# Graph attention's f column: turned in blocks on VectorE and spread over DRAM, in place of TensorE transposes

## The chip, the cores and the metric

The kernel runs on one core of a Trainium2 chip. A core has TensorE (PE: matrix products and transposes; its weight loads are shown apart as PEld), VectorE (DVE), ScalarE (ACT), GpSimd (POOL) and SyncE (SP, which here only issues transfers), each with its own instruction queue that runs in order. They share an on-chip memory of 128 partitions (SBUF); TensorE writes its results to PSUM[...]. Transfers to and from DRAM run on 16 DMA engines. The metric is the time of one execution on the device in microseconds.

## The reference, cut to what matters

There are 64 graphs with 256 nodes and 256 features each, and an adjacency matrix per graph. Four layers follow each other, each wrapped as `x = layernorm(x + layer(x, adj))`: a masked transformer layer, two graph attention layers, and a relational convolution. The change touches the two attention layers. In shortened form:

```python
h = x @ W                             # 256 x 256
f, g = h @ a[0], h @ a[1]             # two numbers for each node
s = leaky_relu(f[:, None] + g[None, :], 0.2)
s = where(adj > 0, s, -inf)
out = softmax(s, axis=-1) @ h
```

Layer 1 adds a bias, layer 2 applies elu. Every score needs one node's f and another node's g.

## The kernel before, in words

A node index is tiled as 2 blocks of 128 partitions (`NB = 2`, `P = 128`, `N = 256`). For each graph, `graph(g)` states every piece of work as an operation of a plan: its engine, an expected cost in microseconds, what it reads and writes, and the ring from which it takes a buffer. `Plan.schedule` then plays the whole program through once, with these costs and with a lag for each engine before others may use a result (for a transfer 3.5 us, unless the operation gives its own `lag`). It starts on each engine the ready operation with the earliest due time, and so writes down the order in which each engine gets its instructions. Graphs follow each other every 46 us by their due times, and the last five are drawn together; at any time several graphs are at different layers, and TensorE takes from all of them. On the chip only this order remains; waiting is done by semaphores.

The attention layer is `gat`. It transposes x (`transposed`, L602 and L605), and makes `h` by products with `gw`, whose weights carry two more columns, so that column `F_COL` of h is f and column `G_COL` is g (L625; copied out of PSUM by ScalarE at L796 in layer 2, by VectorE with a bias at L798 in layer 1). The scores are laid out transposed: keys on the partitions, queries along the free dimension. So g is one number per partition, taken as a scalar operand, and f has to stand as a row on all 128 partitions. Before, TensorE makes that row: `spread` (L807) transposes, for both blocks, the f column repeated 128 times, into a PSUM bank `pf`. VectorE then forms the scores with the mask `gm` in two steps of 128x256 (L812) and applies the leaky slope (L815), ScalarE takes the exponential (L817), and TensorE multiplies h by e (L625 again, bank<-h,e). A further column of ones in h gives the softmax's denominator.

SyncE issues the loads and stores: eight loads of `blocks` per graph for the transposed input (L615), two of `adj` and one each of `x` and `xr` (L578), and the store of the result (L923). GpSimd issues two accumulating transfers per graph (L587), and works on the small operands of the layer norms (L639 to L642). An operation may be marked as using the memory port[...] (`"uses"`), or as waiting for it (`"waits"`); the planner then keeps the marked work of the two engines apart. The turn of 32x32 blocks on VectorE is already in use once per graph, for the input (L618).

Of the kernel before, what the change touches and what calls it, by code (L numbers as in the profile page):

```python
# [17 lines left out]
P = 128  # L18
# [4 lines left out]


RINGS = {"x": 2, "adj": 4, "bits": 2, "am": 2, "gm": 6, "T": 4, "qk": 2, "v": 2, "p": 12, "both": 4, "inv": 1, "ctxT": 2, "X": 8,
         "xr": 1, "hid": 1, "h": 3, "e": 3, "n": 1, "rel": 3, "hi": 2, "lo": 2, "o": 4, "blocks": 1, "xT": 2}
SMALL = {"mv": 8, "st": 4, "rstd": 8, "r": 6, "rdeg": 4}


# [21 lines left out]
class Plan:  # L51
# [29 lines left out]
    def op(self, engine, cost, issue, graph, reads=(), writes=(), takes=(), mode=None, port=None, lag=None):  # L81


        o = Op(engine, cost, mode, graph, issue, port, lag)
        for accesses, writing in ((reads, False), (writes, True)):
            for a in accesses:
                t, part = a if isinstance(a, tuple) else (a, None)
                write = writing
                if t.ring == "bank":
                    write, part = True, None  # L90
                keys = [k for k in t.parts if part is None or k is None or k == part]
                for k in keys:
                    writer, readers = t.parts[k]
                    o.before.update(readers if write else ())
                    if writer is not None:
                        o.before.add(writer)
                if write:
                    if part is None:
                        t.parts = {}
                    t.parts[part] = (o, [])  # L100
                else:
                    for k in keys or [part]:
                        t.parts.setdefault(k, (None, []))[1].append(o)
                if t not in o.tiles and t.ring is not None:
                    o.tiles.append(t)
        o.tiles += [t for t in takes if t not in o.tiles]
        for t in o.tiles:
            t.left += 1
        o.before.discard(o)
        for b in o.before:  # L110
            b.after.append(o)
        self.ops.append(o)
# [96 lines left out]
def tile_gnn_stack(ctx: ExitStack, tc: tile.TileContext, t: dict, out: bass.AP):  # L209
# [16 lines left out]
    nc = tc.nc  # L226
    x_in, adj_in = t["x"], t["adj"]
    B, N, D = x_in.shape
# [3 lines left out]
    NB = N // P  # L232
# [6 lines left out]
    ONE, F_COL, G_COL = D + 2, D, D + 1  # L239
# [5 lines left out]
    pools = {}  # L245
# [42 lines left out]
    def rows(name, zeros=0):  # L288

        v = t[name]  # L290
        n = v.shape[0]
        w = const.tile([P, n + zeros], F32, tag=f"row_{name}", name=f"row_{name}")
        if zeros:
            nc.vector.memset(w[:, n:], 0.0)
        nc.gpsimd.dma_start(w[:, 0:n], bass.AP(tensor=v.tensor, offset=v.offset, ap=[[0, P], [1, n]]))
        return w
# [12 lines left out]
    ident = const.tile([P, P], F32, tag="ident", name="ident")  # L309
# [169 lines left out]
    def main_path(plan):  # L479
# [4 lines left out]
        def ring(name, bufs):  # L484
            plan.ring(name, bufs, lambda shape, dtype, i: pools["work"].tile(shape, dtype, tag=f"{name}{i}", name=name))
# [3 lines left out]
        for name, bufs in SMALL.items():  # L489
            ring(name, bufs)  # L490
        plan.ring("bank", 8, bank)

        c_wqkv, c_wo, c_w1, c_w2, c_b1, c_bo = (plan.fixed(w) for w in (wqkv, wo, w1, w2, b1, bo))
        c_gw, c_cw = [plan.fixed(w) for w in gw], [plan.fixed(w) for w in conv_w]
# [59 lines left out]
        def graph(g):  # L554
            def op(engine, cost, issue, reads, writes, takes=(), mode=None, port=None, lag=None):
                plan.op(engine, cost, issue, g, reads, writes, takes, mode, port, lag)

            def pe(mode, cost, issue, reads, writes, takes=()):
                op("PE", cost, issue, reads, writes, takes, mode)

            def dve(cost, issue, reads, writes, port=None):
                op("DVE", cost, issue, reads, writes, port=port)

            def act(cost, issue, reads, writes):
                op("ACT", cost, issue, reads, writes)
# [4 lines left out]
            def new(ring, shape, dtype=F32):  # L570
                return plan.tile(ring, shape, dtype)

            def tok(ring, dtype=F32):
                return new(ring, [P, NB, D], dtype)
# [20 lines left out]
            def transposed(xt):  # L595

                xT, pt = new("T", [P, KB, N]), new("bank", [P, KB, N])

                def issue():
                    for kb in range(KB):  # L600
                        for i in range(NB):
                            nc.tensor.transpose(pt()[:, kb, i * P : (i + 1) * P], xt()[:, i, kb * P : (kb + 1) * P], ident)  # L602

                pe("full", 0.44, issue, [xt], [pt], [xT])
                act(0.47, lambda: nc.scalar.copy(xT(), pt()), [pt], [xT])  # L605
                return xT
# [15 lines left out]
            def product(dst, lhs, rhs, n):  # L622

                for c in range(n):
                    nc.tensor.matmul(dst, lhsT=lhs(c), rhs=rhs(c), start=(c == 0), stop=(c == n - 1))  # L625
# [161 lines left out]
            def gat(xt, layer, gm, seen, bias, finish):  # L787
                xT = transposed(xt)
                w, c_w = gw[layer], c_gw[layer]
                h, e, z = new("h", [P, NB, HW]), tok("e"), tok("X")  # L790
                for i in range(NB):
                    ph = new("bank", [P, D + 2])
                    pe("full", 0.87, lambda i=i, ph=ph: product(ph(), lambda kb: xT()[:, kb, i * P : (i + 1) * P],
                                                                lambda kb: w[:, kb, :], KB), [xT, c_w], [ph], [h])
                    if bias is None:
                        act(0.27, lambda i=i, ph=ph: nc.scalar.copy(h()[:, i, 0 : D + 2], ph()), [ph], [(h, i)])  # L796
                    else:
                        dve(0.34, lambda i=i, ph=ph: nc.vector.tensor_tensor(h()[:, i, 0 : D + 2], ph(), bias, op=ALU.add),  # L798
                            [ph], [(h, i)])
                pool(0.1, lambda: (nc.gpsimd.memset(h()[:, :, ONE : ONE + 1], 1.0)), [xT], [(h, "one")], None)  # L800
                pool(0.2, lambda: nc.gpsimd.tensor_tensor(seen_fg[:, seen], h()[:, :, F_COL : G_COL + 1],
                                                          h()[:, :, F_COL : G_COL + 1], op=ALU.mult), [(h, 0), (h, 1)], [], "waits")
                pf = new("bank", [P, N])

                def spread():
                    for i in range(NB):
                        nc.tensor.transpose(pf()[:, i * P : (i + 1) * P],  # L807
                                            h()[:, i, F_COL : F_COL + 1].to_broadcast([P, P]), ident)

                pe("full", 0.22, spread, [(h, 0), (h, 1)], [pf], [e])  # L810
                for i in range(NB):
                    dve(0.40, lambda i=i: nc.vector.scalar_tensor_tensor(e()[:, i, :], pf(), h()[:, i, G_COL : G_COL + 1],  # L812
                                                                         gm()[:, i, :], op0=ALU.add, op1=ALU.min),
                        [pf, (h, i), gm], [(e, i)])
                dve(0.60, lambda: nc.vector.scalar_tensor_tensor(e(), e(), SLOPE, e(), op0=ALU.mult, op1=ALU.max), [e], [e],  # L815
                    "uses")
                act(0.52, lambda: nc.scalar.activation(e(), e(), AF.Exp), [e], [e])  # L817
                for i in range(NB):
                    po, r = new("bank", [P, HW]), new("r", [P, 1])
                    pe("full", 0.87, lambda i=i, po=po: product(po(), lambda kt: e()[:, kt, i * P : (i + 1) * P],  # L820
                                                                lambda kt: h()[:, kt, :], NB), [e, h], [po], [z, r])
                    dve(0.08, lambda po=po, r=r: nc.vector.reciprocal(r(), po()[:, ONE : ONE + 1]), [po], [r])
                    finish(i, z, po, r)
                return z
# [82 lines left out]
            xT = input_transposed()  # L907
            adj = load("adj", adj_graph[g], I32)
            am, gm = masks(adj)
# [8 lines left out]
            rel = relation(load("adj", adj_graph[g], I32))  # L918
            rdeg = new("rdeg", [P, NB])
            h = conv(conv(xt, 0, rel, rdeg), 1, rel, rdeg)  # L920
# [7 lines left out]
        for o in plan.schedule():  # L928
            o.issue()

    with tc.tile_pool(name="work", bufs=1) as pools["work"], tc.manual_schedule():
        main_path(Plan())


# [180 lines left out]
    with tc.tile_pool(name="general", bufs=1) as pools["work"], tc.If(wrong > 0):  # L1115
# [11 lines left out]
        with tc.For_i(0, G) as g:  # L1127
            xt = load(gen, x_view[bass.ds(g, 1)], F32, "x")
            xr = load(gen, x_view[bass.ds(g, 1)], F32, "xr")
# [56 lines left out]
```

## Time and profile before

| | |
|---|---|
| median of 3 runs | 2942.13 us (2940.86 to 2942.64) |
| profiled run, span | 2939.3 us |
| TensorE busy | 2894.3 us (98%) |
| VectorE busy | 2415.6 us (82%) |
| ScalarE busy | 1585.1 us (54%) |
| GpSimd busy | 861.4 us (29%) |
| TensorE clock granted | 0.997 of full speed |
| DMA, mean | 49 GB/s |

The span is the time from first to last instruction in the profile. Busy is the time in which at least one instruction of the engine was running. A matrix instruction is pipelined, so its duration from start to end overlaps that of the next one; what the queue pays for it is the distance from its start to the next start. Products in 32-bit floats appear as two records of TensorE for one instruction of the program; transposes appear as one. Lines such as L807 are lines of the kernel's text.

### The profile page before, as it was taken

Reading aid. Unit: us, or ns where it says so; the run is one execution under the profiler, and the core shown is the slowest. Engines: PE = TensorE matmul, PEld = TensorE weight load, DVE = VectorE, ACT = ScalarE, POOL = GpSimd, SP = SyncE. Lnnn points to the kernel's source line nnn. Section 1 sums busy time; section 2 is a strip of 40 time slices with the busy share of each in tenths; the row PEclk is TensorE's granted clock in tenths of the full one; section 3 lists DMA queues with packets and bytes.
Section 4 is the critical chain, followed back from the end, with each engine's and each line's share of the span. In section 5 each row is a group of like instructions: output and inputs, shape, how many; then the busy total and the mean of one; then the engine's idle time right before and its main releaser. Section 6 shows DMA issues by size and latency. Waiting matters only on the chain.

```text
span 2939.3 us, 50120 instructions
## 1 busy us (share of the span) xinstructions
PE 2894.3 (98%) x17206; PEld 2224.7 (76%) x17206; DVE 2415.6 (82%) x6172; ACT 1585.1 (54%) x3841; POOL 861.4 (29%) x2005
## 2 busy tenths in 40 slices
PE   8999999999999999999999999999999999999997
PEld 6777777777777777777777778777777777777884
DVE  6788887888878888878888788878878888889778
ACT  3555554554555556556555555555555555556454
POOL 2233232332322323223233222222332223323232
PEclk9999999999999999999999999999999999999999
DMA  7221121222212222212122212121221212212100
GB/s 179 46 55 44 40 58 38 50 51 47 48 38 51 48 50 44 58 33 58 44 48 48 43 44 62 40 51 44 51 51 40 55 33 51 54 44 48 33 15 23
DMA packets 266037, 143.99 MB, mean 49 GB/s; under 512 B 146960, under 2 KB 264976, under 8 KB 265776
## 3 DMA queue, kind: packets, MB, share of 16 engines
q1 hardware_dynamic: 230336, 105.96, 13.8%
q0 software_dynamic: 35440, 34.76, 8.2%
q8 instruction: 139, 2.28, 0.3%
q14 instruction: 122, 1.00, 0.1%
HBM read 90.32 MB, written 16.78 MB: 36 GB/s over the span
## 4 chain that ended last, share of the span: by engine, by line
PE 84%; DVE 8%; POOL 3%; ACT 2%; issue 1%; DMA 1%; SPq 1%; POOLq 0%; DVEq 0%; ACTq 0%
PE bank L625 66%; PE bank L602 4%; PE bank L887 4%; PE bank L744 3%; PE bank L719 3%; PE bank L739 2%; POOL rstd L640 1%; DVE st L634 1%; ACT X L646 1%; PE bank L807 1%; DVE o L897 1%; DVE X L760 1%; DVE mv L636 1%; DVE p L727 1%; POOL rstd L639 0%
## 5 line engine op out<-in xcount | busy, mean ns | idle before, releaser
L639 POOL TENSOR_SCALAR rstd<-mv 128x2 f32<-128x2 f32 x384 | 108.5, 282 | 1323.0 <-DVE mv L636 1139.2
L625 PE MATMUL bank<-T,w 128*128 128x256 f32 x2048 | 480.0, 380 | 1.1 <-ACT T L605 1.1
L646 ACT ACTIVATE X<-X,rstd 128x256 f32<-128x256 f32 x640 | 349.8, 597 | 231.4 <-POOL rstd L642 164.7
L625 PE MATMUL bank<-cw,T 128*128 128x512 f32 x1024 | 463.6, 595 | 3.7 <-ACT T L605 2.9
L625 PE MATMUL bank<-w,hid 128*128 128x256 f32 x2048 | 462.5, 380 | 0.0
L625 PEld LDWEIGHTS bank<-w,hid 128*128 128x128 f32 x2048 | 383.6, 190 | 54.7 <-issue 4.0
L625 PEld LDWEIGHTS bank<-T,w 128*128 128x128 f32 x2048 | 378.1, 190 | 59.7 <-issue 8.8
L625 PEld LDWEIGHTS bank<-cw,T 128*128 128x128 f32 x1024 | 191.0, 190 | 200.9 <-issue 181.6
L727 DVE TENSOR_TENSOR p<-p,am 128x512 f32<-128x512 f32 x512 | 331.0, 681 | 10.8 <-ACT p L725 10.6
L725 ACT ACTIVATE p<-bank 128x512 f32<-128x512 f32 x512 | 299.1, 596 | 46.4 <-PE bank L719 46.0
L640 POOL TENSOR_TENSOR rstd<-rstd,neghalf 128x2 f32<-128x2 f32 x384 | 303.7, 791 | 32.0
L777 ACT ACTIVATE hid<-bank,col_b 128x256 f32<-128x256 f32 x512 | 213.0, 472 | 117.9 <-PE bank L625 116.2
L625 PE MATMUL bank<-xT,wqkv 128*128 128x256 f32 x1024 | 252.8, 386 | 12.8 <-DVE xT L618 11.5
L605 ACT COPY T<-bank 128x512 f32<-128x512 f32 x320 | 185.1, 586 | 144.2 <-PE bank L602 141.4
L625 PE MATMUL bank<-gw,T 128*128 128x258 f32 x1024 | 249.2, 383 | 1.6 <-ACT T L605 1.5
L625 PE MATMUL bank<-h,e 128*128 128x259 f32 x1024 | 249.0, 383 | 0.9 <-ACT e L817 0.3
L634 DVE BATCH_NORM_STATS2 st<-X 128x6 f32<-128x256 f32 x640 | 237.4, 413 | 1.7
L874 ACT CAST hi<-bank 128x256 fp32r<-128x256 f32 x256 | 94.8, 370 | 256.7 <-PE bank L625 256.1
L748 DVE RECIPROCAL inv<-bank 128x256 f32<-128x256 f32 x128 | 218.7, 1732 | 12.2 <-PE bank L744 12.2
L625 PEld LDWEIGHTS bank<-xT,wqkv 128*128 128x128 f32 x1024 | 188.2, 191 | 49.0 <-DVE xT L618 11.5
L625 PEld LDWEIGHTS bank<-h,e 128*128 128x128 f32 x1024 | 190.5, 190 | 45.8 <-issue 18.4
L625 PEld LDWEIGHTS bank<-gw,T 128*128 128x128 f32 x1024 | 189.7, 190 | 40.0 <-issue 9.1
(120 smaller groups left out, 4997.3 us busy)
## 6 DMA issues: line engine op xcount, KB each, us to landing
adj<-in_adj_dram SPq DMA_DIRECT2D x128, 256.0 KB, 2.8
blocks<-in_x_dram SPq DMA_DIRECT2D x512, 32.0 KB, 2.0
x<-in_x_dram SPq DMA_DIRECT2D x64, 256.0 KB, 2.9
xr<-in_x_dram SPq DMA_DIRECT2D x64, 256.0 KB, 2.7
xr<-row_ln_b POOLq DMA_DIRECT2D x64, 256.0 KB, 4.1
x<-row_bo POOLq DMA_DIRECT2D x64, 256.0 KB, 4.1
out_dram<-o SPq DMA_DIRECT2D x64, 256.0 KB, 2.2
w<-in_W1T_dram SPq DMA_DIRECT2D x1, 1024.0 KB, 12.3
```

The costliest lines, as they stand in the source:

```text
L602: nc.tensor.transpose(pt()[:, kb, i * P : (i + 1) * P], xt()[:, i, kb * P : (kb + 1) * P], ident)
L605: act(0.47, lambda: nc.scalar.copy(xT(), pt()), [pt], [xT])
L625: nc.tensor.matmul(dst, lhsT=lhs(c), rhs=rhs(c), start=(c == 0), stop=(c == n - 1))
L634: nc.vector.bn_stats(stat()[:, i, :], y()[:, i, :])
L639: nc.gpsimd.tensor_scalar(rstd()[:, 0, :], mv()[:, :, 1], 1.0, EPS, op0=ALU.mult, op1=ALU.add)
L640: nc.gpsimd.tensor_tensor(rstd()[:, 0, :], rstd()[:, 0, :], neghalf[:, 0:NB], op=ALU.pow)
L646: nc.scalar.activation(y()[:, i, :], y()[:, i, :], AF.Identity, bias=rstd()[:, 1, i : i + 1], scale=rstd()[:, 0, i : i + 1])
L725: act(0.58, lambda pr=pr, k=k, sr=s[r]: nc.scalar.activation(pr(), sr(), AF.Exp, accum_out=seen_sum[:, k : k + 1]), [s[r]], [pr])
L727: dve(0.60, lambda pr=pr, kt=kt: nc.vector.tensor_tensor(pr(), pr(), am()[:, kt, None, :].to_broadcast([P, KB, N]), op=ALU.mult), [pr, am] ...
L748: dve(1.62, lambda hg=hg, pc=pc: nc.vector.reciprocal(inv()[:, hg, :], pc()[:, 1, :]), [pc], [(inv, hg)])
L777: act(0.36, lambda f=f, k=k, ph=ph: nc.scalar.activation(hid()[:, f + k, :], ph()[:, k, :], AF.Relu, bias=b1[:, f + k : f + k + 1]), [ph, ...
L887: nc.tensor.matmul(pa()[:, 0:n], lhsT=rel()[:, i, j * P : (j + 1) * P], rhs=part()[:, i, 0:n], start=(c == 0), stop=(c == len(terms) - 1))
```

## The change

The row of f is no longer made by TensorE. VectorE turns the f column of each of h's two blocks, repeated 32 times, in blocks of 32x32 into a tile `own` (128 x 64 in all). In it, partition 32 b + r holds f of the nodes 32 b to 32 b + 31 of the block, the same for each r. Two transfers by SyncE write the two halves to a DRAM tile `f_row` of 32 x 256, in which each of the 32 rows is then the whole f. A third reads it back to the tile `f` on 128 partitions, 32 rows four times over. The score step reads f from SBUF and no longer from a PSUM bank[...]. The planner is told a lag of 2.2 us for each write and 4.3 us for the read, in place of its 3.5. The buffer of `e` is taken at the first score step; before, it was taken at the transposes. The rings `f`, `own` and `f_row` have two buffers each. The planner orders all engines' instructions anew with this.

```diff
-         "xr": 1, ..., "o": 4, "blocks": 1, "xT": 2}
+         "xr": 1, ..., "o": 4, "blocks": 1, "f": 2, "own": 2, "xT": 2}
+DRAM = {"f_row": 2}
...
-                pf = new("bank", [P, N])
-                def spread():
-                    for i in range(NB):
-                        nc.tensor.transpose(pf()[:, i * P : (i + 1) * P],
-                                            h()[:, i, F_COL : F_COL + 1].to_broadcast([P, P]), ident)
-
-                pe("full", 0.22, spread, [(h, 0), (h, 1)], [pf], [e])
+                own, rows, pf = new("own", [P, NB * 32]), new("f_row", [32, N]), new("f", [P, N])
+                def turn():
+                    for i in range(NB):
+                        nc.vector.transpose(own()[:, i * 32 : (i + 1) * 32], h()[:, i, F_COL : F_COL + 1].to_broadcast([P, 32]))
+
+                dve(0.22, turn, [(h, 0), (h, 1)], [own], "uses")
+                for i in range(NB):
+                    op("SP", 0.51, lambda i=i: nc.sync.dma_start(rows()[:, i * P : (i + 1) * P].rearrange("r (b n) -> b r n", b=4),
+                                                                 own()[:, i * 32 : (i + 1) * 32]), [own], [(rows, i)], lag=2.2)
+                op("SP", 0.54, lambda: nc.sync.dma_start(pf(), rows()[None, :, :].to_broadcast([4, 32, N])), [rows], [pf], lag=4.3)
                 for i in range(NB):
                     dve(0.40, lambda i=i: nc.vector.scalar_tensor_tensor(e()[:, i, :], pf(), h()[:, i, G_COL : G_COL + 1],
                                                                          gm()[:, i, :], op0=ALU.add, op1=ALU.min),
-                        [pf, (h, i), gm], [(e, i)])
+                        [pf, (h, i), gm], [(e, i)], "uses")
```

More of the change, by code (lines that the diff above doesn't have):

```diff
@@ L25 @@
 RINGS = {"x": 2, "adj": 4, "bits": 2, "am": 2, "gm": 6, "T": 4, "qk": 2, "v": 2, "p": 12, "both": 4, "inv": 1, "ctxT": 2, "X": 8,
-         "xr": 1, "hid": 1, "h": 3, "e": 3, "n": 1, "rel": 3, "hi": 2, "lo": 2, "o": 4, "blocks": 1, "xT": 2}
+         "xr": 1, "hid": 1, "h": 3, "e": 3, "n": 1, "rel": 3, "hi": 2, "lo": 2, "o": 4, "blocks": 1, "f": 2, "own": 2, "xT": 2}
+DRAM = {"f_row": 2}
 SMALL = {"mv": 8, "st": 4, "rstd": 8, "r": 6, "rdeg": 4}
@@ L491, in main_path @@
         plan.ring("bank", 8, bank)
+        for name, bufs in DRAM.items():
+            plan.ring(name, bufs, lambda shape, dtype, i, name=name: pools["dram"].tile(shape, dtype, tag=f"{name}{i}", name=name))
         c_wqkv, c_wo, c_w1, c_w2, c_b1, c_bo = (plan.fixed(w) for w in (wqkv, wo, w1, w2, b1, bo))
@@ L929, in main_path @@
             o.issue()
-    with tc.tile_pool(name="work", bufs=1) as pools["work"], tc.manual_schedule():
+    with (tc.tile_pool(name="work", bufs=1) as pools["work"],
+          tc.tile_pool(name="dram", bufs=1, space=bass.MemoryType.DRAM) as pools["dram"], tc.manual_schedule()):
         main_path(Plan())
```

## The prediction, made before the changed kernel was run

> **What bounds the kernel now.** I read the busy table and the slices first, then TensorE's and VectorE's busy time by stretch, the chain of waits, and last the groups and one stretch in order of time around the two transposes that go.
>
> ```profile
> span 2939.3 us, 50120 instructions
> PE 2894.3 (98%) x17206; PEld 2224.7 (76%) x17206; DVE 2415.6 (82%) x6172; ACT 1585.1 (54%) x3841; POOL 861.4 (29%) x2005
> ...
> PE 84%; DVE 8%; POOL 3%; ACT 2%; issue 1%; DMA 1%; SPq 1%; POOLq 0%; DVEq 0%; ACTq 0%
> ```
> ```profile
> 100.00:2800.00 2700.00, 2685.44 (x16068) 2065.07 (x16067) 2239.99 (x5681) 1475.19 (x3588) 797.92 (x1838) 1.00 0.22 47
> 2800.00:2880.00 80.00, 79.65 (x383) 63.82 (x382) 63.60 (x201) 42.87 (x92) 24.03 (x80) 1.00 0.04 8
> 2880.00:2939.30 59.30, 43.67 (x183) 26.10 (x181) 48.41 (x152) 26.01 (x55) 13.09 (x36) 0.93 0.08 28
> ```
> Columns of the second: stretch, length, then busy us of PE, PEld, DVE, ACT, POOL, the granted clock, the DMA share, GB/s. From 100 to 2800 us TensorE idles 14.6 us of 2700. It is the bound, and a microsecond taken from its queue is a microsecond of span, as long as nothing makes it wait. VectorE has 17% to spare there. Only the last 59 us are different: TensorE 74% busy, VectorE 82%.
>
> What the removed work costs, from the group and then in order of time (start, length):
> ```profile
> L807 PE MATMUL bank<-ident,h 128*128 128x128 f32 x256 | 49.6, 275 | 0.5 <-ACT T L605 0.5
> ...
> 1456.56 0.28 PE L887 MATMUL bank<-hi,rel 128*128 128x256 f32 x1
> 1456.68 0.38 PE L807 MATMUL bank<-ident,h 128*128 128x128 f32 x2
> 1456.89 3.62 PE L625 MATMUL bank<-w,hid 128*128 128x256 f32 x16
> ```
> The 275 ns is one transpose from start to end, and 49.6 us the group's union; both overlap their neighbours. What the queue pays is start to next start: 1456.89 - 1456.68 = 0.21 us for a pair; the pairs at 2871.74 and 2881.67 give 0.22.
>
> What waits for it, and what SyncE has pending:
> ```profile
> DVE e L812 <- PE bank L807: 33.7, 27, 5.4
> ...
> SPq L923 <- ACT o L646: 275.4, 47, 30.5
> ```
> ```profile
> blocks<-in_x_dram SPq DMA_DIRECT2D x512, 32.0 KB, 2.0
> x<-in_x_dram SPq DMA_DIRECT2D x64, 256.0 KB, 2.9
> ```
> Last column: us to landing.
>
> [...] the trace has only the 128x512 one (703 ns). [...] 474 ns for the step with the bank as source, 415 for L843 from SBUF. [...]
>
> **The change, part by part.**
> *Removed:* 2 layers x 64 graphs = 128 pairs x 0.215 us = 27.5 us of TensorE time, all in the saturated part: -27.5. The PSUM bank of the row also falls away; TensorE does not wait for banks before, so 0.
> *VectorE:* 256 turns of 128x32. Not in the trace. From below: the 128x32 memset, 85 ns. [...] I take 0.1 us of queue each (tails overlap), 26 us. The score step now reads SBUF: 256 x (474 - 415) = 15 us less. Net +11 us, bounds +7 to +37, on 2415 with over 500 idle: hidden beside TensorE, 0. [...] the planner keeps GpSimd's small work off them; that work (29% busy) has room.
> *SyncE:* 384 more transfers at some 0.39 us of issue (the trace's median for a load) = 150 us, in a queue that mostly waits. The traffic is 128 x (32 + 128) KB = 21 MB more on 144; the DMA share is 0.22. Hidden, 0. Past what they are moved: loads of blocks, adj, x, xr and the stores, in program order. Counted in the changed program, 69 of 128 row loads have another transfer between the row's writes and its load, mostly a load of blocks; 7 have a store, which waits for ScalarE.
> *The new wait:* from the end of the second h product to the first h x e product. Before, in the stretch above: copy of h to 1456.30 (0.7 us after the products), then the transposes, and 2.8 us from the first score step (1457.28) to the end of the exponential (1460.08). Now, in place of the transposes: turns 0.4, two writes 2 x 0.39 + 2.0, the load 0.39 + 2.7 (the low value for 256 KB), in all 6.3; with what the planner is told (2 x 0.51 + 2.2 + 0.54 + 4.3, and the turns) 8.5. Chain 0.7 + 6.3 + 2.8 = 9.8 us, or 12.0. Against it stands the TensorE work that the new order puts between: I counted its instructions there and priced each by the spacing in the timeline (product of 256 columns 0.434 us, of 512 0.86, transpose 0.11, gather 0.118). Median 14.6 us in the first 116 layers (7 before), 15 of them under 13 and 3 under 12, lowest 9.6. So the chain fits with 2.6 to 4.8 us to spare; I put 2 us in all for the few tight ones (0 to 15).
> *Behind that wait:* VectorE is in order. Between turn and score step lie 7.5 us of its own work at the median, but under 4 in a tenth of the layers; there it stands, and masks, normalisations and the copies of lo behind it stand with it. Its 17% idle pays for that.
> *The end:* of the last 12 layers four have 7.4, 6.1, 8.3 and 7.8 us of TensorE work against a chain of 9.8. The first waits 2.4; the second contains this wait and waits 1.3 more; the third contains both; the last waits 2.0. Sum 5.7 us, with the long chain 14: +6.
> *Start:* the first layer comes at 65 us with 13.6 us of work: 0.
> *Buffers:* h (ring of 3) is held some 7 us longer, twice in a graph's 46 us: room. f, own and f_row have two each, with 23 us between layers.
>
> Sum: -27.5 + 2 + 6 = -19.5, so 2919.8 on the profiled span of 2939.3. The times are some 2.8 us above that span (2942.13 median): 2922.6.
>
> **Rivals.**
> *A, slower: SyncE's order makes the row late.* SyncE's queue is in order and often stands: 47 waits for ScalarE averaged 5.9 us. If one such wait stands ahead of a row's write or load, the row is late, VectorE stops at the score step, and TensorE after it. It decides when TensorE waits over 27.5/128 = 0.21 us per layer beyond what I count, thus once the row takes some 3 us more than planned as a rule. A wait of 1.5 us in a third of the layers costs 64 us: 2942 - 27.5 + 6 + 64 = 2985. For it: 15 row writes stand directly behind a store, 28 behind a load of xr (one buffer). Against: the planner issues a transfer only when it thinks its buffer free, and no load of the before kernel makes TensorE wait after the start.
> *B, no change:* the tail gives 14 and the tight layers 13: 2942. For it: the tail's VectorE is nearly full. Against: it needs the upper end of two terms at once.
> *C, larger gain:* the pair is worth its group's union, 49.6 us: 2942 - 50 + 8 = 2900. Against: the starts, 0.21 us apart, three times.
> *D, the change does nothing for the bound,* VectorE taking over: 2415 + 37 = 2452 us, far under 2890. Out.
>
> **How the numbers follow.** Main case 0.70 (own range 2910 to 2935), C 0.06, B 0.08, A 0.16. Predicted 2923. The range 2905 to 2945 leaves out most of A and half of C. What a measurement of this kernel tells from no change is about 0.2%, 5.9 us: faster 0.76, same 0.08, slower 0.16.
>
> **What would show it.** Right: TensorE's busy time near 2867 us; idle between 100 and 2750 us still under 20 us; score steps on VectorE waiting for the row's transfer in some layers without TensorE waiting; the row's load landing in 2.5 to 4.5 us, its writes in 2; turns at 0.1 to 0.2 us; the score step at about 415 ns; a few microseconds of TensorE idle some 100 us before the end. Wrong: the h x e product on TensorE waiting for the exponential in many layers, with SyncE's row writes behind stores or buffer waits (A), or an end stretch longer by over 10 us (B).

## The result, and the profile after

The changed kernel takes 2954.73 us (median of 4 runs, 2952.18 to 2955.82) against 2941.49 before, a ratio of 1.0044 with a 95% interval of 1.0027 to 1.0061. It is slower by some 13 us, outside the predicted range and of the opposite sign.

The page of the changed kernel, its span, busy table and the chain that ended last:

```profile
span 2953.4 us, 50442 instructions
PE 2886.7 (98%) x16950; PEld 2205.0 (75%) x16950; DVE 2437.8 (83%) x6428; ACT 1583.9 (54%) x3841; POOL 894.7 (30%) x2005
...
PE 81%; DVE 9%; POOL 3%; ACT 3%; issue 2%; DMA 1%; SPq 1%; POOLq 0%; DVEq 0%; ACTq 0%
```

TensorE has 256 records less, as meant, but it is busy only 7.6 us less, where 27.5 were expected, and its idle time (span less busy) has grown from 45.0 to 66.7 us. By stretch, with the columns of the prediction's table:

```profile
100.00:2800.00 2700.00, 2669.68 (x15818) 2040.90 (x15817) 2258.18 (x5911) 1474.02 (x3591) 828.55 (x1839) 1.00 0.24 54
2800.00:2880.00 80.00, 73.52 (x323) 58.76 (x322) 53.47 (x177) 34.66 (x73) 23.46 (x71) 0.94 0.14 31
2880.00:2953.40 73.40, 57.88 (x236) 35.39 (x235) 61.66 (x199) 35.18 (x74) 16.36 (x46) 0.94 0.09 28
```

The steady stretch, which had 14.6 us of TensorE idle, has 30.3. The last product of the transformer layer's scores marks where the end begins, since no new graph enters after it. Here it is before and after (count, shortest, median and longest duration in ns, first and last start):

```profile
L719 PE MATMUL bank<-qk x2048: 373/374/479, 19.1 to 2745.5; 32*128 32x256 f32 x187
```
```profile
L722 PE MATMUL bank<-qk x2048: 374/374/479, 19.8 to 2749.0; 32*128 32x256 f32 x187
```

Up to it the change lost 3.5 us, where some 25 should have been won. From it to the end it went from 193.8 to 204.4 us, 10.6 more.

Whom TensorE waits for, before and after (us in total, times, longest). X is the tile that a layer norm leaves for the next layer:

```profile
PE bank L602 <- ACT X L646: 3.6, 8, 1.3
```
```profile
PE bank L605 <- ACT X L649: 18.7, 33, 1.6
...
PE bank L628 <- ACT e L825: 3.4, 3, 2.0
```

It is not the exponential of the scores (e, 3 waits), behind which the row stands. The largest entry is X, 33 times in place of 8: 15.1 us more, of the 21.7 us by which TensorE's idle time grew. VectorE does stand for the row, but seldom:

```profile
DVE e L820 <- DMA f<-f_row: 19.5, 15, 5.2
```

One stretch with waits for X, 1274 to 1289 us, on TensorE and then GpSimd, in order of time (start, length; in brackets the idle time before it):

```profile
1282.38 2.00 PE L628 MATMUL bank<-xT,wqkv 128*128 128x256 f32 x8
1285.42 0.33 PE L605 MATMUL bank<-ident,X 128*128 128x128 f32 x1 [1.05 <-ACT X L649]
1285.91 0.55 PE L605 MATMUL bank<-ident,X 128*128 128x128 f32 x3 [0.16 <-ACT X L649]
...
1288.32 0.33 PE L605 MATMUL bank<-ident,X 128*128 128x128 f32 x1 [1.64 <-ACT X L649]
```
```profile
1282.98 0.19 POOL L642 TENSOR_SCALAR rstd<-mv 128x2 f32<-128x2 f32 x1 [1.85 <-DVE mv L639]
1283.25 0.70 POOL L643 TENSOR_TENSOR rstd<-rstd,neghalf 128x2 f32<-128x2 f32 x1
1284.03 0.20 POOL L644 TENSOR_TENSOR rstd<-mv,rstd 128x2 f32<-128x2 f32 x1
1284.31 0.19 POOL L645 TENSOR_SCALAR rstd<-rstd 128x2 f32<-128x2 f32 x1
1284.58 0.64 POOL L642 TENSOR_SCALAR rstd<-mv 128x2 f32<-128x2 f32 x1
1285.31 1.03 POOL L643 TENSOR_TENSOR rstd<-rstd,neghalf 128x2 f32<-128x2 f32 x1
1286.41 0.62 POOL L644 TENSOR_TENSOR rstd<-mv,rstd 128x2 f32<-128x2 f32 x1
1287.12 0.51 POOL L645 TENSOR_SCALAR rstd<-rstd 128x2 f32<-128x2 f32 x1
```

GpSimd makes the reciprocal root of a layer norm in four small steps, and ScalarE then makes X with it. Two roots follow each other. The first takes 1.5 us (1282.98 to 1284.50), the second 3.05 us, and X comes after it. On VectorE, meanwhile:

```profile
1284.52 2.46 DVE L730 TENSOR_TENSOR p<-p,am 128x512 f32<-128x512 f32 x4
1286.90 2.49 DVE L734 TENSOR_TENSOR both<-p 128x512 f32<-128x512 f32 x4
```

These are steps with two SBUF inputs, and GpSimd's steps are longer beside them in this trace: the first step of a root (L642) takes 191 ns where it overlaps no step of VectorE (median of 57, at most 193) and 542 ns where it overlaps p<-p,am most (median of 40). Where it overlaps the score step most, it took 191 ns before, when that step read f from a bank (35, at most 193), and takes 331 ns now, with f in SBUF (12). The doubled root agrees with that. It is not shown to be the cause of the waits: the same pair of roots stands ahead of the waits at 1652 and 2016 us, but ahead of that at 793 us the root took 1.7 us, and the kernel before also has roots of over 2.5 us (42 of 384; the changed kernel has 52). VectorE is full in the whole stretch (DVE in the first line below), and the statistics of three layer norms end on it one behind the other from 1281.9 to 1284.6 us:

```profile
1274.00:1288.40 14.40, 11.55 (x81) 8.64 (x79) 14.37 (x43) 10.81 (x29) 8.73 (x17) 1.00 0.24 73
1289.00:1292.40 3.40, 3.40 (x10) 2.77 (x10) 1.14 (x3) 2.29 (x6) 2.54 (x7) 0.51 0.98 145
```

The second line is what comes next: for 3.4 us the granted clock (third number from the end) is 0.51. The starts of TensorE's product records stand 0.43 us apart there, against 0.22 us at 1273 to 1276 us, so work takes twice as long. The trace's record of the clock has 7 such stretches, 27.3 us in all, between the start-up and the last product of the changed kernel; the kernel before has none. Five lie in the steady stretch, each behind waits for X; of the two in the end, one follows a wait for X and one the longest wait for e. Up to 13.7 us of the missing 19.9 us of busy time is this (an estimate, from 27.3/2).

### The profile page after: what moved, and what is told of

Read it like the earlier page. It is cut to its first block, busy times and chain, and to the rows that moved or that the text cites. A ratio compares the mean times of both kernels' runs of the same rounds, so it can differ in the third digit from the quotient of the medians.

```text
span 2953.4 us, 50442 instructions
## 1 busy us (share of the span) xinstructions
PE 2886.7 (98%) x16950; PEld 2205.0 (75%) x16950; DVE 2437.8 (83%) x6428; ACT 1583.9 (54%) x3841; POOL 894.7 (30%) x2005
## 4 chain that ended last, share of the span: by engine, by line
PE 81%; DVE 9%; POOL 3%; ACT 3%; issue 2%; DMA 1%; SPq 1%; POOLq 0%; DVEq 0%; ACTq 0%
PE bank L628 65%; PE bank L605 4%; PE bank L895 4%; PE bank L747 3%; PE bank L722 3%; PE bank L742 2%; POOL rstd L643 1%; DVE st L637 1%; ACT X L649 1%; DVE X L763 1%; DVE inv L751 1%; DVE mv L639 1%; POOL rstd L645 1%; POOL rstd L644 1%; ACT p L728 1%
## 5 line engine op out<-in xcount | busy, mean ns | idle before, releaser
L642 POOL TENSOR_SCALAR rstd<-mv 128x2 f32<-128x2 f32 x384 | 114.9, 299 | 1498.8 <-DVE mv L639 1326.9
L628 PE MATMUL bank<-T,w 128*128 128x256 f32 x2048 | 471.8, 381 | 0.7 <-ACT T L608 0.6
L730 DVE TENSOR_TENSOR p<-p,am 128x512 f32<-128x512 f32 x512 | 334.1, 679 | 18.6 <-ACT p L728 18.3
L643 POOL TENSOR_TENSOR rstd<-rstd,neghalf 128x2 f32<-128x2 f32 x384 | 316.0, 823 | 32.0
L751 DVE RECIPROCAL inv<-bank 128x256 f32<-128x256 f32 x128 | 219.3, 1733 | 22.6 <-PE bank L747 22.2
L628 PEld LDWEIGHTS bank<-xT,wqkv 128*128 128x128 f32 x1024 | 186.9, 191 | 51.3 <-DVE xT L621 12.7
```

The costliest lines, as they stand in the source:

```text
L642: nc.gpsimd.tensor_scalar(rstd()[:, 0, :], mv()[:, :, 1], 1.0, EPS, op0=ALU.mult, op1=ALU.add)
L643: nc.gpsimd.tensor_tensor(rstd()[:, 0, :], rstd()[:, 0, :], neghalf[:, 0:NB], op=ALU.pow)
L730: dve(0.60, lambda pr=pr, kt=kt: nc.vector.tensor_tensor(pr(), pr(), am()[:, kt, None, :].to_broadcast([P, KB, N]), op=ALU.mult), [pr, am] ...
L751: dve(1.62, lambda hg=hg, pc=pc: nc.vector.reciprocal(inv()[:, hg, :], pc()[:, 1, :]), [pc], [(inv, hg)])
```

## The experiments

The theories: **R**, the row comes late (the prediction's rival A); **V**, VectorE's added work, and what it holds up on GpSimd; **O**, the new order of all instructions is worse by itself, within it **M**, through the marks, and **L**, through the lag; **C**, every order is its own draw. Each run is compared with the kernel before, measured beside it (median 2941.5 beside the changed kernel, 2942.9 to 2943.5 beside the others), so differences of 2 to 3 us between rows are not to be relied on. "X waits" are TensorE's waits for a normalised X in the profile (us, times; the kernel before has 3.6, 8). Runs e1, e3, e4, e8 and e11b leave out the row, so their output lacks f.

| run | us | ratio to before, 95% | X waits |
|---|---|---|---|
| changed kernel | 2954.7 | 1.0044 [1.0027, 1.0061] | 18.7, 33 |
| e1 row not read | 2956.1 | 1.0044 [1.0027, 1.0060] | 18.6, 32 |
| e3 order alone | 2949.5 | 1.0023 [1.0013, 1.0034] | 18.3, 35 |
| e5 no marks | 2940.7 | 0.9990 [0.9983, 0.9997] | 7.1, 15 |
| e7 score mark only | 2963.3 | 1.0065 [1.0048, 1.0082] | 14.7, 25 |
| e7b turn mark only | 2950.0 | 1.0022 [1.0015, 1.0029] | 12.0, 25 |
| e8 order alone, no marks | 2939.3 | 0.9983 [0.9974, 0.9991] | 9.8, 18 |
| e9 no marks, shorter lags | 2958.1 | 1.0049 [1.0032, 1.0066] | 10.7, 27 |
| e13 changed, VectorE less | 2948.2 | 1.0016 [1.0009, 1.0023] | 17.3, 33 |
| e4 before, no transposes | 2929.1 | 0.9953 [0.9936, 0.9969] | 5.0, 13 |
| e11 before, VectorE less | 2941.8 | 0.9995 [0.9986, 1.0004] | 2.7, 6 |
| e11b e4, VectorE less | 2926.0 | 0.9938 [0.9921, 0.9954] | 5.2, 12 |
| e6 before, score step marked | 2945.7 | 1.0008 [0.9999, 1.0016] | 7.7, 23 |
| e10 before, other cost | 2945.8 | 1.0005 [0.9997, 1.0014] | 2.8, 9 |
| e12 no marks, last six as before | 2928.5 | 0.9951 [0.9934, 0.9968] | 4.2, 11 |
| e14 the same with marks | 2950.2 | 1.0023 [1.0013, 1.0032] | 15.8, 27 |
| e15 no marks, last nine as before | 2923.7 | 0.9937 [0.9921, 0.9954] | 2.9, 10 |

**Is it the wait for the row?** e1 keeps the changed kernel's plan and all its transfers; only the score step reads something else.

```diff
-  nc.vector.scalar_tensor_tensor(e()[:, i, :], pf(), h()[:, i, G_COL : G_COL + 1],
+  nc.vector.scalar_tensor_tensor(e()[:, i, :], no_f, h()[:, i, G_COL : G_COL + 1],
```


> The changed kernel in its own order, with turns, writes and the load of f all issued, but the score step (VectorE) reads a constant row of zeros in place of f, so that nothing waits for the transfers; the output then lacks f. Changed kernel: 2954.7 us, before: 2941.5. Theory R (the row comes late: VectorE stands 19.5 us in 15 waits for it, and everything behind it on VectorE too): at most 2935, since the waits and most of the 13.7 us that half-clock stretches cost go. Theory O (the new order of all instructions is itself worse; the waits for the row are not what delays TensorE): 2948 to 2957. Theory V (more work on VectorE[...]): 2948 to 2957 too.

2956.1 us, as the changed kernel, with VectorE's 15 waits for the row gone. R has fallen: these waits cost nothing that can be measured, in the end either (204.5 us after the last scores product, against 204.4).

**Is it the order?** e3 also leaves out the turns and the three transfers, in the same plan. Its score step reads the constant row, as in e1 (that edit is not shown again).

```diff
-  dve(0.22, turn, [(h, 0), (h, 1)], [own], "uses")
+  dve(0.22, lambda: None, [(h, 0), (h, 1)], [own], "uses")
   ...
-  op("SP", 0.51, lambda i=i: nc.sync.dma_start(rows()[...], own()[...]), [own], [(rows, i)], lag=2.2)
+  op("SP", 0.51, lambda: None, [own], [(rows, i)], lag=2.2)
```


> As the run with the row not read, and neither turns nor writes nor the load of f are issued: what is left of the change is the removal of TensorE's transposes and the new order. Theory O: 2942 to 2955, slower than or equal to before although TensorE has 27.5 us less to do. Theory V: the 256 turns (0.2 us each from start to end, 51 us as a group's sum at most) and their traffic are gone, so 2915 to 2930. Theory R: the same as the run with the row not read, at most 2935.

2949.5 us: with TensorE's transposes gone and nothing put in their place, the kernel is still slower than before. Its waits for X are those of the changed kernel. The added work thus costs 5 to 7 us (2954.7 and 2956.1 to 2949.5), and the order all the rest. O stands, V only for these few us.

```profile
PE bank L606 <- ACT X L650: 18.3, 35, 1.6
```

**What are the transposes worth?** e4 takes them out of the kernel before and leaves its order alone; its score step too reads a constant row.

```diff
-  pe("full", 0.22, spread, [(h, 0), (h, 1)], [pf], [e])
+  pe("full", 0.22, lambda: None, [(h, 0), (h, 1)], [pf], [e])
```


> The kernel before in its own order, with TensorE's two transposes of f not issued; the score step reads a constant row of zeros from SBUF (output lacks f). It tests the first term of the prediction, 128 pairs x 0.215 us = 27.5 us of a saturated queue: 2914 if each microsecond taken from TensorE is one of span in the old order (all of O, R and V allow it; O needs it). If it is over 2930, the price itself was wrong, since other engines hold TensorE back in any order.

2929.1 us, between the two bounds: a gain of 13.8 us on the 2942.9 of before in this comparison, half of the price. e3 and e4 issue the same number of instructions on every computing engine and differ in the plan that ordered them; the new order alone thus costs 20.4 us. The waits for X in e4 are few:

```profile
PE bank L603 <- ACT X L647: 5.0, 13, 1.4
```

The price itself holds: in the trace of before, the distances from each of the 256 transposes to the next start sum to 31.0 us, with a median of 0.218 us for a pair. In e4, TensorE's busy time is 18.0 us lower than in the profile before and its idle time 6.3 us higher (51.3 against 45.0). Its record of the clock has two stretches at half clock more than before ahead of the end, 6.8 us in the start-up and 3.4 us at 1562 us; they account for up to 5.1 us of the busy time that did not go (an estimate, half of their length).

e11 and e11b ask whether VectorE takes the other half. e11 is the kernel before, e11b is e4, both without the checking step of the relation (L857), 64 of 128x512, so the count that it keeps stays zero.

```diff
-  dve(0.60, lambda: nc.vector.scalar_tensor_tensor(other(), adj(), 1.0, ..., accum_out=seen_rel[:, g : g + 1]), ...)
+  dve(0.60, lambda: None, ...)
```


> The kernel before in its own order, less one VectorE step per graph (64 of 128x512, 0.60 us of queue each, 38 us): the one that only checks the adjacency's values (its count stays zero; the result of the network is complete). Theory T (before, TensorE alone is the bound): 2940 to 2945, no gain from a freer VectorE. Theory S (VectorE shares the bound, by stretches in which it has no idle time): 2925 to 2937.

> The kernel before in its own order without TensorE's transposes of f (2929.1 us; output lacks f), and also less the same VectorE step, 38 us of its queue. It asks where half of the 27.5 us went. Theory S: VectorE takes over as the limit in stretches, so now more of it gets through: 2908 to 2920. Theory T: the rest is lost to something that VectorE does not carry (half clock, startup): 2925 to 2931.

2941.8 and 2926.0 us. With 38 us of planned work less on VectorE's queue, the kernel before gains nothing that can be told from noise (1.5 us, the interval holds 1), and e4 some 3 us, with intervals that overlap. Both lie in the ranges of T: VectorE's total is not a bound in the old order. Beyond the half clock, where the other half goes is spread over many waits of mostly under 1 us and is not settled.

e13 takes the same step out of the changed kernel.

> The changed kernel in its own order, complete but for the same checking step on VectorE (38 us of its queue less). Theory S (in the new order TensorE waits for layer norms that stand in a full VectorE): 2930 to 2945, with TensorE's 18.7 us of waits for normalised X more than halved. Theory P (the layer norms come late because GpSimd's roots were planned late behind the marked steps; VectorE is not what they wait for): 2950 to 2956.

2948.2 us, in the gap between the two expectations. The waits for X stayed (17.3 us, 33 times), against S; what shrank is the time at half clock between start-up and last product, 27.3 to 10.2 us in the record of the clock. The step left out lies in few of the tight stretches (none in 777 to 794 us, one at the start of 1274 to 1288), so this run does not clear VectorE there.

**Is it the marks?** A mark only tells the planner to keep a step of VectorE apart from GpSimd's marked work. e5 takes both away; e7 and e7b leave one.

```diff
-  dve(0.22, turn, [(h, 0), (h, 1)], [own], "uses")
+  dve(0.22, turn, [(h, 0), (h, 1)], [own])
   ...
-                        [pf, (h, i), gm], [(e, i)], "uses")
+                        [pf, (h, i), gm], [(e, i)])
```


> The changed kernel, with the turn and the score step not marked[...], which gives the planner one reason less to move work. All is computed. Theory M (the marks make the planner push GpSimd's layer norm roots back, and TensorE's transposes wait for these: 18.7 us against 3.6 before): 2925 to 2940. Theory O without M: another order with the same latencies, 2945 to 2960. Theory V: as changed or slower[...], 2950 to 2965.

2940.7 us, 14 less than the changed kernel with all its work, and slightly faster than before (20 runs, 2932.7 to 2945.1). The waits for X fell to 7.1 us, as M has it; the time is just above M's range:

```profile
PE bank L605 <- ACT X L649: 7.1, 15, 1.5
```

It is no gain of 27 us either: its last scores product starts at 2734.9 us, 10.6 earlier than before, while the rest takes 203.4 us, 9.6 longer.

> The changed kernel with the mark[...] on the score step only (not on the turn). Both marks: 2954.7 us, none: 2940.7. Theory M1 (the score step's mark, 0.8 us of planned port per layer, is the one that costs): 2950 to 2957. Theory C (each order is its own draw): anywhere from 2932 to 2958.

> The changed kernel with the mark on the turn only. Theory M1 (the score step's mark costs): 2938 to 2944, as with no mark. Theory C: anywhere from 2932 to 2958.

2963.3 and 2950.0 us. Either mark costs, and the score step's alone costs more than both together, so their effects do not add. M1 missed on both: the score step's mark costs more than its range, and the turn's mark is not free. C's span misses the first. Nor are waits for X all that a mark does. In e7, the slowest run, TensorE idles 43.7 us from 100 to 2800 us, and most of that is for other work of ScalarE, the exponentials of the transformer layer (p) and copies (T, h):

```profile
PE bank L605 <- ACT X L649: 12.0, 21, 1.3
PE bank L628 <- ACT p L728: 11.5, 21, 0.7
PE bank L628 <- ACT T L608: 8.0, 12, 1.9
PE bank L605 <- ACT h L799: 7.1, 9, 0.8
```

GpSimd is busy 865.8 us there, against 861.4 before and 894.7 in the changed kernel, so longer work on GpSimd does not explain e7 either.

e6 puts the mark of the score step into the kernel before, and e10 changes one planned cost there (0.22 to 0.26 for the transposes).

> The kernel before with one word added: the score step (which still reads a PSUM bank) is marked[...]. All is computed, no instruction is added or taken away, only the planner's order differs. Theory M (the mark by itself spoils the order: GpSimd's layer norm roots are planned later and TensorE's transposes wait): 2950 to 2960, GpSimd's busy time near 895 us as in the changed kernel, against 861 before. Theory O2 (the mark hurts only together with the row's long lag): 2938 to 2946.

> A control: the kernel before, all the same work, but the planner told 0.26 us in place of 0.22 for TensorE's two transposes of f, which gives another order. Theory C (the orders scatter): off the kernel before by more than 5 us either way. If orders do not scatter: 2939 to 2946.

2945.7 and 2945.8 us, both 2 to 3 us above before; both intervals hold 1. So in the kernel before the score step's mark costs no more than the change of a cost in e10, in O2's range. The marks were seen to cost only with the row in the plan; that its long lag is the reason is not shown. e10 also speaks against C in its plain form: this new order moved the time by less than C's 5 us.

**Is it the lag?** e8 is e3 without marks. e9 is e5 with shorter lags; of its two edits, the first stands for both writes.

```diff
-  [own], [(rows, i)], lag=2.2)
+  [own], [(rows, i)], lag=2.0)
   ...
-  [rows], [pf], lag=4.3)
+  [rows], [pf], lag=3.2)
```


> The order of the run without port marks (2940.7 us), with neither turns, writes nor the load of f issued; the score step reads a constant row (output lacks f). It parts what the new transfers and turns cost from what the order with the longer lag costs, without marks. Theory W (the added work costs, not the order): 2925 to 2931, as the old order without its transposes (2929.1). Theory L (the lag in the plan costs, since each graph takes longer and fewer are ready at a time): 2934 to 2941. With marks the same step was worth 5 us (2954.7 to 2949.5); then 2935.

> Changed kernel without port marks, and the planner told shorter lags for the row: 2.0 us for a write and 3.2 for the load, as the trace shows them, in place of 2.2 and 4.3. All is computed. Theory L (the planned latency costs): 2932 to 2939, better than the 2940.7 without marks. Theory C (every change of a cost in the plan gives another order, good or bad by some 10 us, with no trend): anywhere from 2930 to 2955.

2939.3 us for e8, in L's range: without marks the turns and transfers cost 1.4 us (2940.7 in e5), less than can be told from noise, and the order is still 10 us worse than e4, which issues as many instructions. Whether it is the lag, the planned cost of the new operations or the buffer of `e` that does this was not parted. In its profile the stretch up to the last scores product ends 1.7 us before e4's (2733.2 against 2734.9); the loss is all in the end, 202.1 us against 192.7. e9 is the surprise: 2958.1 us, slower than e5 by 17, far above L's range and just above C's. VectorE stands more for the row:

```profile
DVE e L820 <- DMA f<-f_row: 51.9, 48, 6.1
```

48 waits in place of 14 in e5 (20.3 us). The 3.2 us was too short: where VectorE waited, the score step began 4.1 us (median) after the read's issue in the changed kernel and 4.4 us in e9. So the row is late, as in rival A, but through the plan's optimism and not through stores ahead of it. That these waits are what costs the 17 us is not shown: no run like e1 was made for this plan, the profile is that of the fastest of its four runs (2950.9 us), and TensorE waits for e only 6 times there (4.7 us).

**A better version.** Since the middle gains without marks and the end loses by the plan's longer path for the row, e12 keeps TensorE's transposes for the last six graphs.

```diff
+  if g < B - 6:
       own, rows, pf = ...      # the row over DRAM, unmarked
+  else:
+      pf = new("bank", [P, N])
+      pe("full", 0.22, spread, [(h, 0), (h, 1)], [pf], [e])
```


> A version meant to be faster than both: the row over DRAM without port marks for the first 58 graphs, TensorE's transposes as before for the last six. All is computed. In the run without marks the stretch up to the last scores product was 2714 us against 2726 before, and what follows it 192 against 183. If the last graphs' row latency makes the end longer: 2714 + 183 + start, some 2929 to 2935. If the orders only scatter: 2935 to 2950.

> The version with the row over DRAM in all but the last six graphs (2928.5 us), with both marks put back for those 58 graphs. Theory M (marks cost some 14 us in any order): 2938 to 2946. Theory C: no such step, 2924 to 2934 as likely as slower.

> The version without marks, with TensorE's transposes in the last nine graphs in place of six. If the gain is that of the row's removal in the middle and its absence at the end, the three graphs more cost at most 3 x 2 x 0.215 = 1.3 us: 2927 to 2933. Theory C (it was a lucky order): up to 2945.

e12 takes 2928.5 us, e14 with the marks put back 2950.2, e15 (boundary at nine) 2923.7, which is faster than both kernels with all of the work done: 0.9937 [0.9921, 0.9954] of before. e12 and e15 came out a little below their ranges and e14 above M's, so the sums behind them held in direction only. The stretches of e15:

```profile
100.00:2800.00 2700.00, 2682.92 (x15939) 2064.27 (x15938) 2270.22 (x5924) 1478.62 (x3607) 804.62 (x1854) 1.00 0.25 54
2800.00:2921.20 121.20, 105.77 (x480) 74.60 (x478) 103.25 (x327) 61.09 (x130) 31.84 (x101) 0.96 0.04 14
```

TensorE idles 17.1 us in the steady stretch against 30.3 in the changed kernel, and the end after the last scores product (2728.0 us) is back at 193.2 us. VectorE's load is the same as in the changed kernel, 2437 us. e15 still removes 55 x 2 x 0.215 = 23.7 us of transposes, and 19.5 us of it comes through. The marks cost 22 us between e12 and e14, 14 between e5 and the changed kernel, and 10 between e8 and e3.

## Why the prediction was wrong, point by point

- *The sum.* Forecast were -19.5 us; measured, some +13. By the runs: -13.8 for the transposes in the old order (e4), +20.4 for the new order with the same instructions (e4 to e3; some 10 without the marks, some 10 more with them), and +5 to +7 for the turns and transfers (e3 to the changed kernel and e1).
- *"A microsecond taken from its queue is a microsecond of span, as long as nothing makes it wait."* This step failed first. The price of the pair was right (0.215 us by the starts; 31.0 us for all by the sum in the trace). But with the old order and nothing added, e4, only 13.8 us came through. A busy share of 98% did not show how nearly the other engines only keep up. It is not a fixed half: in e15's order 19.5 of 23.7 us came through, with VectorE's work added.
- *The new wait* was the second step that failed, by what it left out. I counted TensorE's work between the h product and the h x e product in the new order, and found the row's path to fit. That part was right: e1 shows a cost of zero. But it was the only wait of TensorE that I counted; every other chain into TensorE that the planner ordered anew stood at nothing, without a reason. That is the term of +20.4 us, the largest of the sum. The largest part of it that the changed kernel's trace names lies between the statistics of the layer norms and the transposes of X: 18.7 us of waits against 3.6, and half-clock stretches behind the longer of them. This is read from the trace; no run took these waits alone away, and in e7 and e9 the loss lies mostly elsewhere.
- *The marks* I called harmless ("work has room", from GpSimd's 29% busy). That was an average. They cost 10 to 22 us in the three pairs with and without; which part of the planner's choice does it was not isolated.
- *The end.* I put +6, up to 14; it was +10.6, more than the 10 us that I had named as a sign of being wrong. The place was right, the size by luck: my sum was of waits for the row, and e1, in which nothing waits for it, has 204.5 us there. e8 and e3, which have no row at all, have 202.1 and 202.7 against 193.8 before. So it is the plan's path through the last graphs and not the row's real latency; that e15 gets it back shows it. (The 14 also does not follow from the four layers named, which give 10.1 us with the chain of 12.0.)
- *VectorE:* +11 us net, bounds +7 to +37, measured +22.2. The turn takes 190 ns (256 of them, 48.6 us in sum, cover 40.3 us, since neighbours overlap), near the 203 that an estimate from the trace of before gives as an upper bound: 703 ns for the turn of 128x512 (L618), less 480 columns at 1.04 ns, from 682 ns for a step of 512 columns (L815) and 415 for one of 256 (L843). The score step did not get faster from SBUF; its group reads

```profile
L820 DVE SCALAR_TENSOR_TENSOR e<-f,h,gm 128x256 f32<-128x256 f32 x256 | 114.8, 473 | 19.5 <-DMA f<-f_row 19.5
L851 DVE SCALAR_TENSOR_TENSOR n<-n,X 128x256 f32<-128x256 f32 x128 | 52.9, 413 | 0.0
```

  473 ns against 474 from PSUM. I had taken L843 (L851 now), with two f32 inputs, as its like; this step's second tensor is the bf16 mask. Whether that is the reason no run shows. That SBUF is the faster source was thus not shown by the prediction's 474 and 415 ns, which compared unlike steps.
- *SyncE:* nearly hidden: turns and transfers together cost 1.4 us without the marks (e8 to e5) and 5 to 7 with them. Its issues took 0.52 and 0.55 us for the row, not 0.39. The 2.0 us that I put for a write's landing was the median of the loads of blocks in the trace of before (1.6 to 7.2). In the changed kernel the row's read is issued 2.0 us (median of 128, at least 1.9) after the start of the second write's issue. The order around one row shows loads of blocks between write and load, without harm:

```profile
1042.04 1.14 SPq L816 DMA_DIRECT2D f_row<-own  x2
1045.06 0.87 SPq L618 DMA_DIRECT2D blocks<-in_x_dram  x2
1046.02 0.55 SPq L818 DMA_DIRECT2D f<-f_row  x1
```

- *Rival A* had the right sign and 16% for it, but its mechanism does not work in the changed kernel (e1). At most it has a part in e9, where the planner was told less than the row takes. The rival that came true, an order that is worse by itself, was not on my list.

## What to carry to other kernels

Where a planner writes the order, a change of one operation changes every queue; before trusting a saved microsecond, count the work between producer and consumer in the new order for all chains that end in the bounding engine, not only for the one that was edited. (That this count would have given the 20 us was not tried.) To part the order from the work, keep the plan and issue nothing for the new operations: that one run told here that the order alone was slower than the kernel before. A longer planned path that the middle of a program hides was paid at its end, so let the last rounds keep the short path.

## What the hardware showed that I had not expected

TensorE dropped to half clock for 3.4 or 6.8 us after short lulls (granted clock 0.51 from 1289.0 to 1292.4 us). In the stretch shown, the 5.05 us between the end of one group of products (1284.38) and the start of the next (1289.43) hold only 3.0 us of idle time, in pieces of at most 1.64, the rest being transposes. All seven drops of the changed kernel come at the end of stretches of 2.0 to 5.1 us without a product, in which TensorE idled 1.5 to 3.0 us. So there several short waits around transposes stood ahead of a drop, in place of one long one, and a drop of 3.4 us cost up to 1.7 us beyond the wait itself (an estimate, half its length). Five more such stretches, of 2.1 to 2.7 us, passed without a drop, so their length alone does not decide it.
